# Four GNN layers on one core: where the first attention stripes' row work runs, layer 0's row buffers, and the order of the roots

## The chip, the cores and the metric

The kernel runs on one core of a Trainium2 chip. The metric is device time in microseconds (us), the median of three executions. Next to the times there is one execution recorded by the hardware profiler. Its engines are PE (TensorE, matmuls), DVE (VectorE), ACT (ScalarE), POOL (GpSimd) and SP (SyncE, which here issues the loads of the adjacency matrix). L1119 means line 1119 of the kernel.

## The reference

N = 4096 nodes with D = 64 features and a dense 0/1 adjacency matrix of float32. Four layers, each followed by a residual sum and a layer norm over the features:

```python
# layer 0
deg = clip(sum(adj, 1) + 1, 1)
h = (adj @ x + x) / deg
z = relu(concat([x, h]) @ W + b)
out0 = z / max(norm(z), 1e-12)
# layers 1 and 3 (c = 1 / r**2 in layer 1, c = 1 in layer 3)
x_t = logmap0(x, c)
left, right = x_t @ w_att[:D], x_t @ w_att[D:]
a = sigmoid(left[:, None] + right[None, :] + b_att) * adj
out = proj(expmap(x, einsum('ij,ijd->id', a, logmap(x[:, None], x[None], c))))
# layer 2: the last 100 neighbours of a row, weighted 0.5 ** (rank from the end)
out2 = w @ (x @ weight) + bias
# after each layer
x = layernorm(x + out, eps=1e-5)
```

So every attention layer needs, per pair of nodes (i, j), a sigmoid and a function of the distance in the hyperbolic space, and per node some scalars: squared norms, reciprocals, roots and logarithms.

## The kernel before

The nodes stand in 4 groups of 1024 (`GROUPS`, worked from 3 down to 0) and 32 blocks of 128. The adjacency matrix is streamed in tiles of 1 MB, `edges`, 256 of them, from SP into a pool of six buffers. Layers 0 and 2 are matmuls of edges with node features, with PE's and ACT's order written out by hand (`manual_schedule`). In the attention layers (1 and 3) that order is left to the scheduler, which keeps close to the order of the program.

**An attention stripe** (`attend`, L1064) is one group of target nodes against all 32 blocks. The blocks come in 16 pairs, highest first, and each block is a tile of 128 x 1024 scores. For one tile PE writes six matmuls into one of three PSUM buffers `z` (L1098, L1101, L1104), ACT makes a sigmoid `sig` (L1113) and a square `sq` (L1116), and DVE makes `t = max(z, 0) * sig` (L1119). For a pair DVE then makes `t = (sq + H²) * t` (L1121, 128 x 2048), and two pairs later PE adds t up with the features of the blocks (`acc`, L1076). At a stripe's end ACT copies acc out as `sums` (L1127).

**Row work** is what is done per node: 1024 nodes are a tile of 128 x 8 x 64, that is 128 x 512 features or 128 x 8 scalars. It is written as generators whose steps are issued between the tiles: `tick(n)` (L616) lets queued generators go on, and a generator that yields k rests for k ticks. The tick rate per tile is 2 in the first stripe of layer 1, 4 in the first stripe of layer 3, and 1 elsewhere, with one more call per pair. `need` (L643) runs ticks until a group is ready, before the first pair that reads it. How many ticks a generator rests is told by helpers: `soon`, `near`, `after(small)` and `pool_done`.

A layer's last group (group 0) is finished while the next layer's first stripe is already running on the blocks of groups 3, 2 and 1; so for layers 1 and 3 the following runs inside that first stripe: `end_0` (L1408) or `end_2` (L1540), which end layer 0 or 2; then `norm_rows` (L894), the layer norm; then `prepare` (L914), which makes the scalars and the operands of attention. `prepare` computes `y` (features scaled), its two-part representation in f16 (`ys`, `yd`), `xe` (the operand of L1076), then four transposes on PE (L978), each followed by a copy by ACT (L982) into `hi_lo`, `lo_hi`, `src` and `dst`; then two logarithms by ACT (L986, L987, which need another activation table than the sigmoid), a product on PE with the attention vectors (L991), and `left` and `right`. In attention the PSUM pool of these transposes (`aux`) has a single buffer.

**Roots** are computed from a bit trick and three Newton steps. `rsqrt` (L720) is on DVE: 1 + 3 x 3 instructions on 128 x 8. The class `Small` (L733) holds scalar row work that runs on DVE or on GpSimd; its `rsqrt` (L757) takes 1 + 3 x 3 on DVE, or the seed on DVE and 3 x 4 on GpSimd. The work at the end of each attention stripe (`move`, L1137) uses it.

**Buffers.** Pool `row` holds row tiles by name, one buffer each unless told otherwise. In layer 0 `own` holds the operands `first` and `third`, the sums of layer 0's own rows `xw`, the weights `sum_w` and `count_w`, and the scratch tile `junk`; a pool `m0_sb` holds `top` and `low`, copies of layer 0's sums. Both are closed at the end of layer 0, and the attention pool `p_sb` (sq, t, sig) then takes the same part of SBUF. A pool that takes another's place waits, through the dependences of its bytes, for the readers of what stood there.

Of the kernel before, what the change touches and what calls it, by code (L numbers as in the profile page):

```python
# [10 lines left out]
F32 = mybir.dt.float32  # L11
# [39 lines left out]
LN2 = 0.6931471805599453  # L51
ROOT2 = 2.0**0.5
LOG = (0.3333341, 0.1998662, 0.14984541)
OFF_EDGE = 255.0
# [6 lines left out]
def gnn_stack_kernel(  # L61
# [509 lines left out]
    def stream(fits):  # L571

        with ExitStack() as st:
# [89 lines left out]
            def pool_done(small, large=0):  # L663
# [3 lines left out]
                return 2 + int(small * 0.33 + large)  # L667

            spare, turn_of = [], [0]

# [49 lines left out]
            def rsqrt(a, name):  # L720

                n = a.shape[1]
                r, t = nums(name, n), nums("rs_t", n)
                V.tensor_scalar(
                    r.bitcast(I32), a.bitcast(I32), -0.5, float(0x5F3759DF), ALU.mult, ALU.add
                )
                for _ in range(3):
                    V.tensor_mul(t, r, r)
                    V.scalar_tensor_tensor(t, t, -0.5, a, ALU.mult, ALU.mult)
                    V.scalar_tensor_tensor(r, t, 1.5, r, ALU.add, ALU.mult)  # L730
                return r

            class Small:  # L733
# [23 lines left out]
                def rsqrt(self, a, name, small):  # L757

                    r, t = self.nums(name), self.nums("rs_t")
                    if self.on_pool:  # L760
                        yield self.wait(small)
                    V.tensor_scalar(
                        r.bitcast(I32), a.bitcast(I32), -0.5, float(0x5F3759DF),
                        ALU.mult, ALU.add,
                    )
                    for _ in range(3):
                        self.mul(t, r, r)
                        if self.on_pool:
                            self.mul(t, t, a)
                            self.ts(t, t, -0.5, 1.5, ALU.mult, ALU.add)  # L770
                            self.mul(r, t, r)
                        else:
                            self.stt(t, t, -0.5, a, ALU.mult, ALU.mult)
                            self.stt(r, t, 1.5, r, ALU.add, ALU.mult)
                    return r
# [39 lines left out]

            def att_rows(w_att, name):

                t = row.tile([1, 2, 2, D], F32, name=name + "_row")
                src = w_att.rearrange("(u d) o -> o u d", u=2)
                nc.scalar.dma_start(t, src[:, :, None, :].to_broadcast([1, 2, 2, D]))  # L820
                return t
# [72 lines left out]
            def norm_rows(layer, s, v, x2_to):  # L894

                m, v2, sq = nums("n_m"), nums("n_v2"), grp("sq")
                V.tensor_reduce(m, v, AX.X, ALU.add)
                V.tensor_scalar(m, m, 1.0 / D, None, ALU.mult)
                yield soon()
                V.tensor_sub(v, v, over(m))  # L900
                nc.gpsimd.tensor_mul(sq, v, v)  # L901
                yield soon()
                yield soon()
                V.tensor_reduce(v2, sq, AX.X, ALU.add)
                yield soon()
                V.tensor_scalar(m, v2, 1.0 / D, 1e-5, ALU.mult, ALU.add)
                r = rsqrt(m, "n_r")
                yield soon()
                V.tensor_mul(x_of(layer)[:, blocks(s), :], v, over(r))
                V.tensor_mul(x2_to, r, r)  # L910
                V.tensor_mul(x2_to, x2_to, v2)
                yield soon()

            def prepare(layer, s, att, b_att, curve, least, good, small):  # L914
# [4 lines left out]
                xg, bg, rbg = x_of(layer)[:, at, :], b[:, at], rb[:, at]  # L919
                V.tensor_scalar(cx2[:, at], x2[:, at], c, None, ALU.mult)  # L920
                V.tensor_scalar(bg, cx2[:, at], -1.0, 1.0, ALU.mult, ALU.add)
                V.reciprocal(rbg, bg)

                V.tensor_scalar(rbg, rbg, -0.13, 0.0, ALU.max, ALU.min)

                ym, y = nums("ym"), grp("y")
                V.tensor_scalar(ym, rbg, sc, None, ALU.mult)
                V.tensor_mul(y, xg, over(ym))

                def second():  # L930
# [12 lines left out]
                    for k, of in ((7, 0), (8, 0), (9, 1)):  # L943
                        nc.gpsimd.tensor_scalar(
                            ed[:, :, k], hl[:, :, of], -2.0 / UNIT, None, ALU.mult
                        )
                    V.tensor_sub(ys[:, :, D : 2 * D], y, ys[:, :, :D])

                    m, g, w = nums("m"), nums("g"), grp("xw")
                    V.tensor_scalar(g, cx2[:, at], 1.0, 1.0 / D, ALU.add, ALU.mult)  # L950
                    V.tensor_scalar(m, rbg, CUBE / UNIT, None, ALU.mult)
                    yield 1
                    V.tensor_add(w, xg, over(g))
                    yield 1
                    V.tensor_mul(xe[:, at, :], w, over(m))

                    q, q1, t = nums("q"), nums("q1"), nums("tt")
                    V.tensor_scalar(q, x2[:, at], least, c, ALU.max, ALU.mult)
                    V.tensor_scalar(q1, q, SMALL, None, ALU.max)
                    rt = rsqrt(q1, "rt")  # L960
                    V.tensor_mul(t, q1, rt)
                    V.tensor_scalar(t, t, TOP, None, ALU.min)
                    V.tensor_scalar(q1, q1, QTOP, None, ALU.min)
                    by_log = layer == 3 and s != GROUPS[-1]
                    if by_log:
                        half_log_of_ratio(t, q1)
                    yield 2 * near()
                    for into, rows_of in (
# [61 lines left out]

                later(second(), True, after(small))
                yield 1
# [321 lines left out]
            with ExitStack() as lp:  # L1354
                own = lp.enter_context(tc.tile_pool(name="m0_own", bufs=1))
                sb = lp.enter_context(tc.tile_pool(name="m0_sb", bufs=2))
                ps = lp.enter_context(tc.tile_pool(name="m0_ps", bufs=6, space=PSUM))
# [6 lines left out]
                third = own.tile([P, NB, D + 1], BF16, name="third")  # L1364
                xw = own.tile([P, NB, D], F32, name="xw")
                sum_w = own.tile([P, D + 1], F32, name="sum_w")
                count_w = own.tile([D + 1, D + 1], F32, name="count_w")
                ident_b = own.tile([P, P], BF16, name="ident_b")
# [32 lines left out]
                nc.scalar.dma_start(sum_w[:D, :D], w0[D:, :])  # L1401
                att_rows1, att_rows3 = att_rows(w_att1, "att1"), att_rows(w_att3, "att3")

# [4 lines left out]
                def end_0(s, tops):  # L1408
# [29 lines left out]
                    V.tensor_scalar(n2, n2, 1e-24, None, ALU.max)  # L1438
                    n = rsqrt(n2, "n")
                    yield 1  # L1440
                    V.tensor_mul(z, z, over(n))
                    V.tensor_add(z, z, x0[:, blocks(s), :])
                    yield 1
                    yield from norm_rows(1, s, z, x2[:, blocks(s)])
# [4 lines left out]
                with tc.manual_schedule(engines=FIXED):  # L1449
                    for s in GROUPS:  # L1450
# [37 lines left out]
                        for h in range(2):  # L1488
                            top = sb.tile([P, W], F32, name="top")
                            nc.scalar.copy(top, sums[h])  # L1490
                            low = sb.tile([D + 1, W], F32, name="low")
                            nc.scalar.copy(low, counts[h][: D + 1])
                            tops.append((top, low))
# [183 lines left out]
            with tc.manual_schedule(engines=FIXED):  # L1677
                spare.append(of_third)

                for some in (GROUPS[:2], GROUPS[2:3], GROUPS[3:]):  # L1680
                    accs = wide_pass(some) if len(some) == 2 else narrow_pass(some[0])
                    for s, of in zip(some, accs):
                        sums = [row.tile([P, W], F32, name="sums", bufs=2) for _ in of]
                        for to, acc in zip(sums, of):
                            nc.scalar.copy(to, acc)
                        later(end_2(s, sums))
# [98 lines left out]
```

## Time and profile before

| | us |
|---|---|
| median of 3 executions (1074.15 to 1074.6) | 1074.26 |
| the profiled execution | 1069.06 |
| its span on the core | 1067.3 |
| first score matmul of layer 1 | 185.02 |
| last stripe of layer 1 closed (L1127) | 517.38 |
| first score matmul of layer 3 | 714.08 |
| last stripe of layer 3 closed (L1127) | 1038.34 |

The mean granted clock of TensorE was 0.971 of full. Busy shares over the span, from the page's first part: PE 92%, DVE 86%, ACT 71%, POOL 25%. A share is an average over four stages with different limits, so stages are read one by one below. In a profile's timeline each line has the start, the duration, the engine, the line of the kernel, the operation, out<-in with shapes, how often it is repeated, and in brackets how long the engine stood idle before it and who released it.

```profile
PE   5997998789999999999999999998899999999980
DVE  8577887899999999999485489849999999999976
POOL 0011212010044515435500010101102454444163
PEclk8899999989999999999999999999999999999985
```

These are busy tenths in 40 slices of 26.7 us. Slices 7 to 19 (from 0) are layer 1's attention, 26 to 38 layer 3's. In the first stripe of each, GpSimd has almost nothing to do; in the other stripes it works on the rows of the stripe before.

### The profile page before, as it was taken

To read this page: it belongs to the slowest core of one execution; us is meant where nothing else is said; L and a number is where in the kernel's file an instruction comes from. 1 tells how busy PE (TensorE), PEld (TensorE's weight loads), DVE (VectorE), ACT (ScalarE), POOL (GpSimd) and SP (SyncE) were. 2 spreads that over 40 slices of the span, in tenths; PEclk is the share of its full clock that TensorE was granted. 3 is DMA by queue.
4 is the path that set the end of the run, shared out by engine and by line. 5 is a ranking of instruction groups with operands and counts; after the bars stand their busy time and mean duration, and the time that the engine had idled before them with its cause. 6 is when DMAs were issued, how large, how long until landed. Compare 5 with 4: busy or idle time off the path is not lost.

```text
span 1067.3 us, 13569 instructions
## 1 busy us (share of the span) xinstructions
PE 982.1 (92%) x4760; PEld 403.2 (38%) x4845; DVE 920.2 (86%) x1501; ACT 754.3 (71%) x877; POOL 270.8 (25%) x649
## 2 busy tenths in 40 slices
PE   5997998789999999999999999998899999999980
PEld 2454554333333333333333344443333333333320
DVE  8577887899999999999485489849999999999976
ACT  0013122779988899888677788898898888898850
POOL 0011212010044515435500010101102454444163
PEclk8899999989999999999999999999999999999985
DMA  9999999745656656757598999996465766666300
GB/s 364 356 426 364 383 395 375 277 175 197 233 204 230 215 206 202 249 184 249 205 363 332 371 346 316 324 321 222 138 236 190 250 216 208 241 228 234 131 1 24
DMA packets 38580, 271.62 MB, mean 254 GB/s; under 512 B 4710, under 2 KB 4710, under 8 KB 5734
## 3 DMA queue, kind: packets, MB, share of 16 engines
q1 hardware_dynamic: 37728, 270.03, 69.3%
q8 instruction: 40, 0.66, 0.2%
q10 hardware_dynamic: 774, 0.63, 0.2%
q14 instruction: 38, 0.31, 0.1%
HBM read 269.58 MB, written 1.05 MB: 254 GB/s over the span
## 4 chain that ended last, share of the span: by engine, by line
PE 66%; DVE 22%; ACT 5%; DMA 2%; POOL 2%; issue 2%; ACTq 0%; SPq 0%; POOLq 0%
PE acc L1076 17%; PE z L1641 11%; PE z L1101 8%; PE z L1098 7%; PE z L1104 7%; DVE t L1119 7%; DVE t L1121 6%; PE acc L1465 6%; PE z L1653 3%; DVE junk L844 2%; PE z L1607 2%; DMA edges<-in_adj_dram 2%; ACT sq L1648 1%; ACT sq L1116 1%; POOL sq L1435 1%
## 5 line engine op out<-in xcount | busy, mean ns | idle before, releaser
L1119 DVE SCALAR_TENSOR_TENSOR t<-z,sig 128x1024 f32<-128x1024 f32 x256 | 309.7, 1218 | 16.9 <-ACT sq L1116 14.9
L1121 DVE SCALAR_TENSOR_TENSOR t<-sq,t 128x2048 f32<-128x2048 f32 x128 | 295.2, 2306 | 0.2
L1116 ACT ACTIVATE sq<-z 128x1024 f32<-128x1024 f32 x256 | 254.3, 1021 | 56.5 <-PE z L1104 21.6
L1113 ACT ACTIVATE sig<-left_b,right 128x1024 f32<-128x1024 f32 x256 | 286.9, 1149 | 5.3 <-DVE t L1119 4.5
L1076 PE MATMUL acc<-t,xe 128*64 128x512 f32 x1024 | 260.4, 614 | 10.9 <-DVE t L1121 9.3
L1101 PE MATMUL z<-lo_hi,hi_lo 128*128 128x512 f16 x512 | 193.7, 378 | 3.8 <-issue 0.9
L1104 PE MATMUL z<-dst,src 74*128 74x512 f16 x512 | 194.7, 380 | 0.0
L1098 PE MATMUL z<-edges,two_i 128*128 128x512 bf16 x463 | 181.7, 392 | 5.4 <-DVE t L1119 5.4
L1648 ACT ACTIVATE sq<-z 128x512 bf16<-128x512 f32 (+1 forms) x192 | 137.6, 740 | 40.1 <-PE z L1641 39.5
L1076 PEld LDWEIGHTS acc<-t,xe 128*64 128x64 f32 x1024 | 64.3, 137 | 140.6 <-issue 106.5
L1098 PEld LDWEIGHTS <-two_i 128*128 128x128 bf16 x512 | 50.2, 98 | 120.7 <-issue 74.5
L1465 PE MATMUL acc<-edges,first 128*128 128x512 bf16 x241 | 77.9, 400 | 16.5 <-DMA edges<-in_adj_dram 15.9
L1641 PE MATMUL z<-edges,pass_by 128*128 128x512 bf16 x240 | 84.7, 388 | 7.3 <-ACT sq L1648 6.0
L844 DVE SCALAR_TENSOR_TENSOR t<-edges 128x2048 bf16<-128x2048 f32 x32 | 73.0, 2287 | 19.6 <-DMA edges<-in_adj_dram 19.2
L1641 PE MATMUL z<-edges,enter 128*128 128x512 bf16 x251 | 86.8, 387 | 0.5
L844 DVE SCALAR_TENSOR_TENSOR junk<-edges 128x2048 bf16<-128x2048 f32 x32 | 73.1, 2284 | 13.1 <-DMA edges<-in_adj_dram 13.1
L1465 PE MATMUL acc<-edges,third 128*65 128x512 bf16 x256 | 80.9, 397 | 0.8 <-issue 0.2
L1104 PEld LDWEIGHTS <-src 74*128 74x128 f16 x512 | 49.1, 96 | 72.0 <-issue 9.2
L1101 PEld LDWEIGHTS <-hi_lo 128*128 128x128 f16 x512 | 50.2, 98 | 60.6 <-issue 14.5
L901 POOL TENSOR_TENSOR sq<-z 128x512 f32<-128x512 f32 x8 | 10.2, 1278 | 156.1 <-DVE z L900 144.8
L1184 POOL TENSOR_TENSOR w_att<-x,u 128x512 f32<-128x512 f32 x6 | 12.7, 2121 | 140.9 <-ACT u L1179 140.9
L1607 PE MATMUL z<-sq,halves 128*128 128x512 bf16 x120 | 45.1, 377 | 0.7 <-ACT sq L1648 0.5
(399 smaller groups left out, 965.0 us busy)
## 6 DMA issues: line engine op xcount, KB each, us to landing
edges<-in_adj_dram SPq DMA_DIRECT2D x256, 1024.0 KB, 4.9
x<-in_x_dram SPq DMA_DIRECT2D x4, 256.0 KB
out_dram<-x ACTq DMA_DIRECT2D x2, 256.0 KB
out_dram<-x SPq DMA_DIRECT2D x2, 256.0 KB
w_sb<-in_L_gnn_W_dram ACTq DMA_DIRECT2D x1, 32.0 KB, 4.8
w_twice<-in_L_gnn_weight_dram ACTq DMA_DIRECT2D x2, 16.0 KB, 4.8
given<-in_L_gnn_b_dram ACTq DMA_DIRECT2D x1, 0.2 KB
given<-in_L_gnn_bias_dram ACTq DMA_DIRECT2D x1, 0.2 KB
```

The source lines that it names most:

```text
L844: V.scalar_tensor_tensor(junk, a, 0.0, a, ALU.not_equal, ALU.not_equal, accum_out=odd[:, n : n + 1])
L1076: it = nc.tensor.matmul(acc[h * D : (h + 1) * D, :], xe[:, j, :], t[:, k, h * W : (h + 1) * W], start=j == BLOCKS[0], stop=j == BLOCKS[-1],)
L1098: nc.tensor.matmul(half, two_i, edge[:, at : at + W], start=True, stop=False)
L1101: nc.tensor.matmul(half, hi_lo[:, of], lo_hi[:, to], start=False, stop=False)
L1104: last = nc.tensor.matmul(half, src[:, of], dst[:, to], start=False, stop=True)
L1113: nc.scalar.activation(sig, left_b, AF.Sigmoid, bias=right[:, j : j + 1])
L1116: nc.scalar.activation(sq[:, k], zp, AF.Square, bias=ROOT + OFF, scale=-1.0 / UNIT)
L1119: V.scalar_tensor_tensor(t[:, k], zp, 0.0, sig, ALU.max, ALU.mult)
L1121: V.scalar_tensor_tensor(t, sq, HIGH**2, t, ALU.add, ALU.mult)
L1465: nc.tensor.matmul(accs[h][:m], lhs[:, j, :], edge[:, at : at + W], start=j == BLOCKS[0], stop=j == BLOCKS[-1],)
L1641: nc.tensor.matmul(z[:, h : h + W], lhs, rhs[:, h : h + W], start=j == BLOCKS[0], stop=True, skip_group_check=True,)
L1648: weighed[0] = nc.scalar.activation(w, z[:, :n], AF.Exp, bias=-(OFF_EDGE + CUT) * LN2, scale=-LN2)
```

## The change

There are four edits.

1. Layer 0's row buffers: `xw` lies in the tile `halves`, `sum_w` and `count_w` in the pool that is never closed, `top` and `low` in row tiles (`sums`, `w_att`, `u_1`), the attention vectors' row in the tile `xw` of `row`. Pool `m0_sb` is gone.
2. For the last group, `end_0`, `norm_rows` and `prepare` issue on GpSimd most of the 128 x 512 steps and many scalar steps, and use the root of `Small` on GpSimd. New rests `far(small, large)` stand where the results are used.
3. All roots take one step of third order and one Newton step: 1 + 7 instructions on DVE, the seed on DVE and 10 on GpSimd.
4. Layer 2's sums of the last group are copied by DVE rather than ACT.

```diff
+THIRD = 0.375**0.5
...
+            def far(small, large=0):
+                beat = {1: 0.8, 3: 0.4}.get(place[0], 1.6)
+                return 1 + int((small * 0.29 + large * 1.04 + 2.3) / beat)
...
             def rsqrt(a, name):
-                for _ in range(3):
-                    V.tensor_mul(t, r, r)
-                    V.scalar_tensor_tensor(t, t, -0.5, a, ALU.mult, ALU.mult)
-                    V.scalar_tensor_tensor(r, t, 1.5, r, ALU.add, ALU.mult)
+                V.tensor_mul(t, r, r)
+                V.scalar_tensor_tensor(t, t, THIRD, a, ALU.mult, ALU.mult)
+                V.scalar_tensor_tensor(t, t, -10.0 / 3.0 * THIRD, t, ALU.add, ALU.mult)
+                V.scalar_tensor_tensor(r, t, 5.0 * THIRD**2, r, ALU.add, ALU.mult)
+                V.tensor_mul(t, r, r)
+                V.scalar_tensor_tensor(t, t, -0.5, a, ALU.mult, ALU.mult)
+                V.scalar_tensor_tensor(r, t, 1.5, r, ALU.add, ALU.mult)
...
             class Small:
...
                 def rsqrt(self, a, name, small):
...
+                    if self.on_pool:
+                        s = self.nums("rs_s")
+                        self.mul(t, t, a)
+                        self.ts(s, t, 0.375, -1.25, ALU.mult, ALU.add)
+                        self.mul(t, t, s)
+                        self.ts(t, t, 1.875, None, ALU.add)
+                        self.mul(r, t, r)
                         self.mul(t, r, r)
+                        self.mul(t, t, a)
+                        self.ts(t, t, -0.5, 1.5, ALU.mult, ALU.add)
+                        self.mul(r, t, r)
...
             def norm_rows(layer, s, v, x2_to):
...
+                pooled = s == GROUPS[-1]
+                E = nc.gpsimd if pooled else V
                 yield soon()
-                V.tensor_sub(v, v, over(m))
+                E.tensor_sub(v, v, over(m))
                 nc.gpsimd.tensor_mul(sq, v, v)
-                yield soon()
-                yield soon()
+                if pooled:
+                    yield far(0, 2)
+                else:
+                    yield soon()
+                    yield soon()
...
-                r = rsqrt(m, "n_r")
-                yield soon()
-                V.tensor_mul(x_of(layer)[:, blocks(s), :], v, over(r))
-                V.tensor_mul(x2_to, r, r)
-                V.tensor_mul(x2_to, x2_to, v2)
-                yield soon()
+                if pooled:
+                    r = yield from Small(True, "").rsqrt(m, "n_r", 0)
+                else:
+                    r = rsqrt(m, "n_r")
+                    yield soon()
+                E.tensor_mul(x2_to, r, r)
+                E.tensor_mul(x2_to, x2_to, v2)
+                E.tensor_mul(x_of(layer)[:, blocks(s), :], v, over(r))
+                if not pooled:
+                    yield soon()
...
             def prepare(layer, s, att, b_att, curve, least, good, small):
...
-                V.tensor_scalar(cx2[:, at], x2[:, at], c, None, ALU.mult)
-                V.tensor_scalar(bg, cx2[:, at], -1.0, 1.0, ALU.mult, ALU.add)
+                E.tensor_scalar(cx2[:, at], x2[:, at], c, None, ALU.mult)
+                E.tensor_scalar(bg, cx2[:, at], -1.0, 1.0, ALU.mult, ALU.add)
+                if pooled:
+                    yield far(14, 1)
                 V.reciprocal(rbg, bg)
-                V.tensor_scalar(rbg, rbg, -0.13, 0.0, ALU.max, ALU.min)
+                E.tensor_scalar(rbg, rbg, -0.13, 0.0, ALU.max, ALU.min)
-                V.tensor_scalar(ym, rbg, sc, None, ALU.mult)
-                V.tensor_mul(y, xg, over(ym))
+                E.tensor_scalar(ym, rbg, sc, None, ALU.mult)
+                E.tensor_mul(y, xg, over(ym))
...
-                    V.tensor_sub(ys[:, :, D : 2 * D], y, ys[:, :, :D])
+                    E.tensor_sub(ys[:, :, D : 2 * D], y, ys[:, :, :D])
-                    V.tensor_add(w, xg, over(g))
-                    V.tensor_mul(xe[:, at, :], w, over(m))
+                    E.tensor_add(w, xg, over(g))
+                    E.tensor_mul(xe[:, at, :], w, over(m))
...
-                    rt = rsqrt(q1, "rt")
-                    V.tensor_mul(t, q1, rt)
-                    V.tensor_scalar(t, t, TOP, None, ALU.min)
-                    V.tensor_scalar(q1, q1, QTOP, None, ALU.min)
+                    if pooled:
+                        rt = yield from Small(True, "").rsqrt(q1, "rt", 0)
+                    else:
+                        rt = rsqrt(q1, "rt")
+                    E.tensor_mul(t, q1, rt)
+                    E.tensor_scalar(t, t, TOP, None, ALU.min)
+                    E.tensor_scalar(q1, q1, QTOP, None, ALU.min)
-                    yield 2 * near()
+                    yield far(10, 1) if pooled else 2 * near()
...
-                later(second(), True, after(small))
+                later(second(), True, far(2, 1) if pooled else after(small))
...
                 own = lp.enter_context(tc.tile_pool(name="m0_own", bufs=1))
-                sb = lp.enter_context(tc.tile_pool(name="m0_sb", bufs=2))
-                xw = own.tile([P, NB, D], F32, name="xw")
-                sum_w = own.tile([P, D + 1], F32, name="sum_w")
-                count_w = own.tile([D + 1, D + 1], F32, name="count_w")
+                xw = halves.bitcast(F32)
+                sum_w = keep.tile([P, D + 1], F32, name="sum_w")
+                count_w = keep.tile([D + 1, D + 1], F32, name="count_w")
...
                 def end_0(s, tops):
...
-                    n = rsqrt(n2, "n")
-                    yield 1
-                    V.tensor_mul(z, z, over(n))
-                    V.tensor_add(z, z, x0[:, blocks(s), :])
-                    yield 1
+                    if s == GROUPS[-1]:
+                        n = yield from Small(True, "").rsqrt(n2, "n", 0)
+                        nc.gpsimd.tensor_mul(z, z, over(n))
+                        nc.gpsimd.tensor_add(z, z, x0[:, blocks(s), :])
+                        yield far(10, 2)
...
-                            top = sb.tile([P, W], F32, name="top")
+                            top = row.tile([P, W], F32, name="sums", bufs=2)
...
                         for to, acc in zip(sums, of):
-                            nc.scalar.copy(to, acc)
+                            if s == GROUPS[-1]:
+                                V.tensor_copy(to, acc)
+                            else:
+                                nc.scalar.copy(to, acc)
```

## The prediction

> **What bounds the kernel now.** I read the page first (busy times, chain, groups), then the ACT timeline at each end of a stripe, then DVE, ACT, PE and POOL side by side over the two first attention stripes (185–287 and 714–810 us), and last the end of the program.
>
> ```profile
> PE 66%; DVE 22%; ACT 5%; DMA 2%; POOL 2%; issue 2%; ACTq 0%; SPq 0%; POOLq 0%
> ...
> L1119 DVE SCALAR_TENSOR_TENSOR t<-z,sig 128x1024 f32<-128x1024 f32 x256 | 309.7, 1218 | 16.9 <-ACT sq L1116 14.9
> L1121 DVE SCALAR_TENSOR_TENSOR t<-sq,t 128x2048 f32<-128x2048 f32 x128 | 295.2, 2306 | 0.2
> ```
>
> The chain runs over PE and DVE. In a steady attention stripe they are level: a pair of tiles costs DVE two L1119 (start to start 1.13) and one L1121 (2.20), 4.46 us, and PE twelve matmuls of 0.22 and 1.87 for L1076, about 4.6 us. So in attention anything put into DVE's or PE's order is paid for, unless the stripe has slack. How much the first stripes lose is read from the copies that close stripes one and two of layer 1, and one and two of layer 3:
>
> ```profile
> 287.05 0.58 ACT L1127 COPY sums<-acc 128x512 f32<-128x512 f32 x1
> ...
> 364.09 0.59 ACT L1127 COPY sums<-acc 128x512 f32<-128x512 f32 x1
> ...
> 809.77 0.59 ACT L1127 COPY sums<-acc 128x512 f32<-128x512 f32 x1
> ...
> 886.49 0.59 ACT L1127 COPY sums<-acc 128x512 f32<-128x512 f32 x1
> ```
>
> A steady stripe takes 77.0 and 76.7 us, 2.4 a tile. The first ones, from their first score matmul (185.02 and 714.08), take 102.0 and 95.7 for about 36 tiles' worth, some 86. So about 16 and 10 us are excess, and only these can be won in attention. Where they lie in layer 1:
>
> ```profile
> 189.31 1.28 ACT L1113 ACT_TABLE_LOAD   x1 [5.31 <-DVE z L1429]
> ```
> ```profile
> 194.93 0.39 PE L1098 MATMUL z<-edges,two_i 128*128 128x512 bf16 x1 [3.72 <-DVE t L1119]
> ...
> 229.57 0.62 PE L978 MATMUL aux<-ident,ys 128*128 128x128 f16 x8 [1.96 <-DVE ys L947]
> 231.29 1.01 PE L978 MATMUL aux<-ident,ys 128*128 128x128 f16 x8 [1.10 <-ACT hi_lo L982]
> ```
> ```profile
> 242.10 0.21 DVE L1001 TENSOR_REDUCE lr<-aux 128x16 f32<-128x48 f32 x1 [3.71 <-PE aux L991]
> ```
>
> The first: ACT stands 5.31 us before its first sigmoid, whose buffer lies where layer 0's xw lay, which DVE's L1429 reads. The others: PE waits for scores, then for the last group's row batch (225.81 to 229.90 on DVE), and the transposes go one by one through a single buffer that ACT empties.
>
> The price of GpSimd is in the POOL timeline of a later stripe:
>
> ```profile
> 311.67 0.20 POOL L771 TENSOR_TENSOR r_t<-rs_t,r_t 128x8 f32<-128x8 f32 x1
> 311.95 2.24 POOL L767 TENSOR_TENSOR rs_t<-r_t 128x8 f32<-128x8 f32 x1
> 314.26 0.20 POOL L769 TENSOR_TENSOR rs_t<-rs_t,t 128x8 f32<-128x8 f32 x1
> ...
> 363.40 1.04 POOL L1266 TENSOR_TENSOR u<-u,q 128x512 f32<-128x512 f32 x1
> 364.52 3.11 POOL L1269 TENSOR_TENSOR x<-u,w_att 128x512 f32<-128x512 f32 x1
> ```
>
> A small operation takes 0.20 (0.28 to the next), but 2.24 when it meets L1121 on DVE; a large one 1.04, or 3.11.
>
> **What the Trainium skill says.** "SBUF — State Buffer", Who interferes with whom: a DVE instruction with two SBUF inputs and a GpSimd instruction that reads SBUF exclude each other, whoever starts first. The trace agrees: L1121 (both inputs in SBUF) gives the 2.24, L1119 (z in PSUM) does not. So GpSimd loses some 2.2 of every 4.6 us, and L1121 can be held by a large GpSimd operation too (3.16 instead of 2.28 at 363.43). "GPSIMD Engine Reference", 3.1 Elementwise: an add takes 1.96 times as long as on DVE; here 1.04 against 0.69, 1.5 times.
>
> **The change, part by part.** Times are of the profiled execution (1069.06; span 1067.3, 1.8 around it). The median 1074.26 is 5.2 above it; I keep that distance.
>
> *Layer 0's buffers.* The sigmoid buffers no longer overlie what L1429 reads. ACT's last copy ends at 184.0, the table load (1.28) at 185.3, the first sigmoid at 186.35, the square at 187.3. DVE's order still has z's finish (to 189.1) ahead of the first L1119, so that goes from 193.66 to 189.1, 4.5 earlier; the root's ten instructions (191.76 to 193.58) are no longer ahead of it. The other overlays (junk, first) are read earlier; I take no new wait from them.
>
> *Last group on GpSimd, layer 1.* In DVE's new order three of its instructions wait for GpSimd with scores queued behind them: the mean's sum (L897 before), the variance's sum (L904) and the reciprocal (L922); further on the attention factor (L1006) waits for ACT's logarithm, whose input now comes from a GpSimd root. DVE is in order, so each late result stops the scores, and through them PE. Writing u1, u2, ... for the L1121s and stepping with 1.13, 2.20, 0.08 (small) and 0.60 (large):
> u1 192.45 (before 197.85), u2 197.9 (205.15). The root is seeded at 196.0: six of its ten GpSimd steps fit before u2, the seventh waits to 200.1, three more to 201.0, then two large ones to 203.1. DVE comes free at 201.3, so the mean's sum stops it 1.9. u3 206.2 (211.19). The subtract and square stop it 0.9: u4 212.35 (215.89), u5 216.8 (220.59). The next root meets u4 and u5 (2.8 + 2×2.0), then x, x2 and 1−cx² (0.28 each, 1.04 for x): the reciprocal waits until 221.3, 2.4 idle; u6 223.2 (229.90). Before, DVE's batch cost 4.1 there. The low half of ys comes from GpSimd at 229.25 behind u6; PE's transposes therefore wait at 227.3–229.3, as before. u7 229.2 (233.54), u8 234.35 (242.50); the transposes now lie between four tiles, so the 3.71 stop goes, while the logarithm and its two table loads (245.57–249.4 before) come at about 241–244. u9 241.6 (247.41). The twentieth L1119 ends at 248.0 against 252.63: **−4.6**. So the 4.5 of the buffers survives, and moving row work nets about nothing: about 7.8 us of DVE work go (one root 2.0, two spread ones 0.8 each, seven large ones of 0.6), and 5.2 of stops, transposes held for ys and steps that DVE did while it would have waited for PE anyway come.
>
> *Last group on GpSimd, layer 3.* Here no buffer wait is won; ticks are twice as dense, so the same waits come after fewer tiles. DVE's sums copies (two, 0.6 each) and the bias add that waits for PE stand ahead of the first L1119: 719.1 against 718.67. u1 722.9 (722.36); subtract and square stop DVE 1.2; u2 730.6 (728.09). The root needs 2.8 plus a 2.0 block, then about six more operations before the reciprocal: stop 3.5, u3 737.6 (735.52). The low half of ys (742.0–743.05) holds u4: 743.05 (740.22). u5 749.2 (744.91), u6 752.75 (750.21). The third root meets both, ACT's logarithm waits to 756.5, DVE behind it 2.7: u7 763.05 (757.72). Then it gains: the batch of 4.1 is gone and transposes are past. At u10's tile it is 780.1 against 778.4: **+1.7**.
>
> *Third order.* Seven dependent steps after the seed instead of nine on DVE, ten instead of twelve on GpSimd. In the tail's chain three DVE roots stand in a row with 0.20 a step:
>
> ```profile
> 1047.16 0.90 DVE L767 TENSOR_TENSOR rs_t<-r_t 128x8 f32<-128x8 f32 x1
> ...
> 1055.33 0.17 DVE L767 TENSOR_TENSOR rs_t<-n 128x8 f32<-128x8 f32 x1
> 1055.53 0.17 DVE L747 SCALAR_TENSOR_TENSOR rs_t<-rs_t,mt 128x8 f32<-128x8 f32 x1
> ```
>
> 3×2×0.20 = 1.2, and half of one GpSimd root at 1037–1042 (2×0.28, of which ACT's copy at 1042.4 lets 0.3 through): **−1.5**. The three steps stretched to 0.9–1.0 by GpSimd's L1265–L1269 remain. In layer 0 (DMA busy share 0.92 to 0.99) and layer 2 (PE) shorter roots are hidden: 0, at most −0.5. In steady stripes a root sheds at most 2 of 0.08 from DVE: below 0.3.
>
> *Sums by DVE.* ACT gives up 2×0.5 at 716.66, but is not late there: 0 beyond the 0.4 counted.
>
> Sum −4.6 + 1.7 − 1.5 = −4.4: span 1062.9, profiled 1064.7, median 1069.9. Unknown costs: a GpSimd result may slip before or behind one L1121, 2.2 each way, at the seven or so waits of the two stripes; a net of two in one direction is ±4, which I take.
>
> **Rivals.**
> (1) GpSimd hides better: its operations fall between the L1121s and the layer 3 stops (1.2 + 3.5 + 2.7) shrink to half. For: GpSimd stands idle from 202 to 227 now. Against: the groups are dependent chains longer than the 2.4 us gap. −4.4 − 3.7: about 1066. 15%.
> (2) In-order DVE behind blocked GpSimd, the slower side: one more 2.2 block at the reciprocal and at the factor in both stripes, +8.8, PE idle with its clock dropping to 0.8 as at 220–240. For: every root is longer than a gap. Against: before also had a 3.7 stop there that goes. −4.4 + 8.8: 1078.7. It decides from 6.5 us of added stops. 13%.
> (3) The buffers do not free ACT: another overlay (junk, the first operand) still orders the first sigmoid behind layer 0's end. Then 0 + 1.7 − 1.5, within 0.2% (2.15 us, about what a measurement can tell from no change): 1074.5. Against: the profile names L1429 alone. 15%.
>
> **How the numbers follow.** Forecast 57%, own range 1067.5–1073; rivals 15, 13, 15%. The range 1066 to 1077 takes in (1)'s value and (3), and reaches towards (2). Faster by over 0.2% (below 1072.1): nearly all of (1), most of the forecast: 0.70. Within: 0.17. Slower: (2), 0.13.
>
> **What would show it.** Table load at 184 instead of 189.31 and first L1119 near 189.1; first stripe's closing copy near 282.4, the second stripe still 77.0 later; in layer 3 95.7 + 1.7 us; DVE idle with POOL as releaser about 5 us in layer 1 and 7 in layer 3; from the last closing copy to the end 1.5 shorter than 29.0 us. Wrong if stripes two to four change by over 1 us, if the first L1119 stays near 193, or if POOL stops sum to over 18 us.

## The result and the profile after

| | before | changed |
|---|---|---|
| median of 7 executions each, side by side | 1074.06 (1070.35 to 1074.6) | 1069.25 (1064.74 to 1074.99) |
| ratio, 95% interval | | 0.9972 [0.9948, 0.9996] |
| profiled execution, span | 1069.06, 1067.3 | 1068.74, 1067.0 |

The change is faster by 0.28%, and the interval's upper end, 0.9996, is nearly no change. The forecast, 1069.9, is met by the median; the profiled pair differs by only 0.3 us. So the stages have to be read one by one. Lines have moved: in the changed kernel L1160 and L1162 are L1119 and L1121 of before, L1117 is L1076, L1139 is L1098 and L1019 is L978; in the other kernels they are a few lines off these. The chain of the changed kernel has moved from DVE to PE and GpSimd:

```profile
PE 70%; DVE 16%; ACT 5%; POOL 4%; DMA 4%; issue 2%; ACTq 0%; SPq 0%; POOLq 0%
```

The copies that close stripes one and two of layer 1, and one and two of layer 3 (ACT timeline):

```profile
286.77 0.59 ACT L1168 COPY sums<-acc 128x512 f32<-128x512 f32 x1
...
363.75 0.59 ACT L1168 COPY sums<-acc 128x512 f32<-128x512 f32 x1
...
810.83 0.59 ACT L1168 COPY sums<-acc 128x512 f32<-128x512 f32 x1
...
887.81 0.59 ACT L1168 COPY sums<-acc 128x512 f32<-128x512 f32 x1
```

The first score matmuls stand at 182.92 and 713.19. From there the first stripes take 103.9 us (before 102.0) and 97.6 (95.7); the second ones 77.0 each (77.0 and 76.7). From layer 3's first closing copy to the end it is 256.2 instead of 257.5. Layer 1 did not gain its 4.6 (its first closing copy stands at 286.77, not near 282.4), although the wait that was to go is gone, as the ACT timeline shows:

```profile
181.92 1.28 ACT L1154 ACT_TABLE_LOAD   x1
...
191.55 1.02 ACT L1157 ACTIVATE sq<-z 128x1024 f32<-128x1024 f32 x1 [4.18 <-PE z L1145]
```

The table load has no idle time before it (5.31 before). But the second square now waits 4.18 us for PE, whose granted clock is 0.50 just there, from 184 to 190 us of this execution (PE timeline; the same matmul takes 0.39 at full clock, 0.63 here):

```profile
182.92 0.39 PE L1139 MATMUL z<-edges,two_i 128*128 128x512 bf16 x1
...
183.73 0.63 PE L1139 MATMUL z<-edges,two_i 128*128 128x512 bf16 x1
```

After that come the forecast stops of DVE (its timeline: mean's sum, variance's sum, reciprocal, each released by POOL), and then one that was priced too low (PE timeline: the first transposes wait for the low half of ys, and the next sums of L1117 take 3.22 us for eight matmuls, not 1.94):

```profile
205.78 0.69 DVE L920 TENSOR_REDUCE n_m<-z 128x8 f32<-128x512 f32 x1 [1.86 <-POOL z L1482]
...
211.94 0.69 DVE L932 TENSOR_REDUCE n_v<-sq 128x8 f32<-128x512 f32 x1 [0.93 <-POOL sq L926]
...
224.06 0.20 DVE L958 RECIPROCAL rb<-b 128x8 f32<-128x8 f32 x1 [2.23 <-POOL b L955]
```
```profile
231.03 1.03 PE L1019 MATMUL aux<-ident,ys 128*128 128x128 f16 x8 [4.15 <-POOL ys L983]
232.00 3.22 PE L1117 MATMUL acc<-t,xe 128*64 128x512 f32 x8
```

Layer 3 shows its stops where the forecast put them (DVE timeline), and the third root on GpSimd held by two L1162s (POOL timeline, its usual 0.20 grown to 2.36), with the low half of ys at 3.20:

```profile
726.40 0.69 DVE L932 TENSOR_REDUCE n_v<-sq 128x8 f32<-128x512 f32 x1 [1.22 <-POOL sq L926]
...
736.52 0.20 DVE L958 RECIPROCAL rb<-b 128x8 f32<-128x8 f32 x1 [3.70 <-POOL b L955]
...
756.57 0.17 DVE L1050 SCALAR_TENSOR_TENSOR f<-q,tt 128x8 f32<-128x8 f32 x1 [1.87 <-ACT q L1028]
```
```profile
741.27 3.20 POOL L983 TENSOR_TENSOR ys<-y,ys 128x512 f16<-128x512 f32 x1 [0.73 <-DVE hl L971]
...
752.32 2.36 POOL L786 TENSOR_TENSOR rt<-rs_t,rt 128x8 f32<-128x8 f32 x1
```

### The profile page after: what moved, and what is told of

Same layout as the page of the kernel before. It is cut to its first block, busy times and chain, and to the rows that moved or that the text cites. A ratio compares the mean times of both kernels' runs of the same rounds, so it can differ in the third digit from the quotient of the medians.

```text
span 1067.0 us, 13581 instructions
## 1 busy us (share of the span) xinstructions
PE 986.4 (92%) x4845; PEld 402.8 (38%) x4845; DVE 902.7 (85%) x1380; ACT 753.0 (71%) x875; POOL 305.6 (29%) x695
## 4 chain that ended last, share of the span: by engine, by line
PE 70%; DVE 16%; ACT 5%; POOL 4%; DMA 4%; issue 2%; ACTq 0%; SPq 0%; POOLq 0%
PE acc L1117 18%; PE z L1693 11%; PE z L1139 9%; PE z L1145 8%; PE z L1142 8%; PE acc L1511 5%; DVE t L1160 4%; DVE t L1162 4%; DMA edges<-in_adj_dram 3%; PE z L1705 3%; PE z L1659 2%; DVE junk L867 2%; ACT sq L1700 1%; ACT sq L1157 1%; PE aux L1209 1%
## 5 line engine op out<-in xcount | busy, mean ns | idle before, releaser
L1160 DVE SCALAR_TENSOR_TENSOR t<-z,sig 128x1024 f32<-128x1024 f32 x256 | 309.9, 1219 | 21.1 <-ACT sq L1157 18.5
L1162 DVE SCALAR_TENSOR_TENSOR t<-sq,t 128x2048 f32<-128x2048 f32 x128 | 295.2, 2306 | 0.3
L1117 PE MATMUL acc<-t,xe 128*64 128x512 f32 x1024 | 258.9, 615 | 13.9 <-DVE t L1162 13.0
L1139 PE MATMUL z<-edges,two_i 128*128 128x512 bf16 x512 | 201.4, 393 | 5.9 <-DVE t L1160 5.9
L1117 PEld LDWEIGHTS acc<-t,xe 128*64 128x64 f32 x1024 | 63.8, 137 | 144.3 <-issue 103.8
L1511 PE MATMUL acc<-edges,first 128*128 128x512 bf16 x256 | 80.3, 395 | 16.5 <-DMA edges<-in_adj_dram 16.2
L1139 PEld LDWEIGHTS <-two_i 128*128 128x128 bf16 x512 | 50.6, 99 | 117.4 <-issue 71.9
L1659 PE MATMUL z<-sq,halves 128*128 128x512 bf16 x128 | 48.1, 377 | 0.6 <-ACT sq L1700 0.6
## 6 DMA issues: line engine op xcount, KB each, us to landing
x<-in_x_dram SPq DMA_DIRECT2D x4, 256.0 KB
out_dram<-x ACTq DMA_DIRECT2D x2, 256.0 KB
out_dram<-x SPq DMA_DIRECT2D x2, 256.0 KB
```

The source lines that it names most:

```text
L1117: it = nc.tensor.matmul(acc[h * D : (h + 1) * D, :], xe[:, j, :], t[:, k, h * W : (h + 1) * W], start=j == BLOCKS[0], stop=j == BLOCKS[-1],)
L1139: nc.tensor.matmul(half, two_i, edge[:, at : at + W], start=True, stop=False)
L1160: V.scalar_tensor_tensor(t[:, k], zp, 0.0, sig, ALU.max, ALU.mult)
L1162: V.scalar_tensor_tensor(t, sq, HIGH**2, t, ALU.add, ALU.mult)
L1511: nc.tensor.matmul(accs[h][:m], lhs[:, j, :], edge[:, at : at + W], start=j == BLOCKS[0], stop=j == BLOCKS[-1],)
```

## The experiments

Theory: the steps of the prediction, buffers −4.5, handover neutral in layer 1 and costly in layer 3. Rival: in layer 1 the handover gives back what the buffers win. Each ratio is to the kernel before, timed beside it. Since layer 0's end alone lies anywhere from 182.9 to 190.6 us in the profiled executions, the table counts stripes from the first score matmul, each in one profiled execution. Rows with the same code in a stage show the scatter of that stage.

In brackets stands how much of a stripe PE spent at half clock. The granted clock is 1.00 or 0.50 in these stretches, so a slice of 1 us with a mean of 0.75 counts as 0.5 us.

| kernel | ratio to before, 95% | first stripe, layer 1 (of it at half clock) | first stripe, layer 3 (of it at half clock) | from there to the end |
|---|---|---|---|---|
| before | 1 | 102.0 (10.2) | 95.7 (3.4) | 257.5 |
| changed | 0.9972 [0.9948, 0.9996] | 103.9 (17.1) | 97.6 (3.4) | 256.2 |
| buffers alone | 1.0013 [0.9993, 1.0032] | 101.1 (3.4) | 95.4 (3.4) | 257.7 |
| roots alone | 0.9965 [0.9950, 0.9980] | 102.4 (13.7) | 96.1 (3.4) | 255.9 |
| buffers and roots | 0.9938 [0.9920, 0.9957] | 98.7 (3.4) | 95.9 (3.4) | 255.9 |
| no handover | 0.9913 [0.9889, 0.9937] | 99.9 (6.8) | 93.2 (0) | 256.0 |
| handover in layer 1 | 0.9949 [0.9930, 0.9967] | 100.9 (10.2) | 94.4 (6.8) | 256.0 |
| handover in layer 3 | 0.9963 [0.9949, 0.9978] | 97.2 (0) | 97.3 (10.2) | 256.2 |
| end_0 only | 0.9891 [0.9872, 0.9909] | 98.0 (6.8) | 95.7 (6.8) | 255.8 |
| low half back | 0.9905 [0.9881, 0.9930] | 95.4 (0) | 95.7 (3.4) | 256.0 |
| low half alone | 0.9945 [0.9920, 0.9970] | 99.2 (3.4) | 95.6 (6.8) | 256.1 |
| low half back, layer 1 | 0.9899 [0.9864, 0.9935] | 98.0 (6.8) | 94.4 (3.4) | 256.0 |
| second half, layer 1 | 0.9981 [0.9956, 1.0005] | 106.7 (17.1) | 94.1 (3.4) | 255.9 |
| second half, both | 1.0032 [1.0014, 1.0050] | 103.3 (10.2) | 100.1 (13.6) | 255.8 |

**Buffers alone.** Edit 1 on the kernel before.

> The kernel before with edit 1 alone (layer 0's row buffers). Theory of the prediction: ACT's first sigmoid no longer waits, first L1119 near 189 instead of 193.66, and the gain lasts: the first stripe of layer 1, from its first score matmul to its closing copy, takes about 97.5 instead of 102.0 us, layer 3's stays at 95.7, the end at 29.0; total -4.5 us against before (ratio about 0.996). Rival (the gain is taken back in the same stripe by the row batch and the serial transposes, which then come at an earlier tile): stripe 101 to 102, total within 1 us of before.

The first stripe took 101.1 and the ratio is 1.0013: the theory's 97.5 did not come. The early part is as expected: the first L1119 (L1123 in this kernel) follows the first score matmul by 4.1 us instead of 8.6. Then the gain is lost at one place (ACT timeline; the logarithm, its copies of `left` for the next stripe, and the way back to the sigmoid):

```profile
258.19 1.28 ACT L990 ACT_TABLE_LOAD   x1
259.48 0.21 ACT L990 ACTIVATE tt<-tt 128x8 f32<-128x8 f32 x1
...
261.45 0.59 ACT L1064 COPY left_b<-aux 128x512 f32<-128x512 f32 x1 [1.66 <-PE aux L1058]
...
263.65 0.59 ACT L1064 COPY left_b<-aux 128x512 f32<-128x512 f32 x1 [0.52 <-PE aux L1058]
264.25 1.28 ACT L1117 ACT_TABLE_LOAD   x1
```

ACT does no sigmoid from 253 to 265.5, and DVE stands 4.29 us before its next L1123. In ACT's order the logarithm stands behind the 24th sigmoid here, behind the 19th in the kernel before: the scores went ahead and the rows, a root step per tile, did not, so the logarithm ran into the next stripe's `left`.

**No handover, and handover in one layer.**

```diff
-                pooled = s == GROUPS[-1]
+                pooled = False
...
-                    if s == GROUPS[-1]:
+                    if False:
```

In the kernels for one layer the first condition has `and layer == 1` or `and layer == 3` instead, and end_0's own belongs to layer 1.

> The changed kernel without edit 2: the last group's rows stay on VectorE in both attention layers; buffers, third-order roots and sums by VectorE stay. Theory of the prediction (handover neutral in layer 1, +1.7 in layer 3): layer 1's first stripe as in the changed kernel within 1 us, layer 3's 95.7 instead of 97.6, end 27.6; total 2 us below the changed kernel. Rival (in layer 1 the handover gives back what the buffers win): layer 1's first stripe about 98 instead of 103.9, so 5 to 7 us below the changed kernel, ratio to before about 0.993.

> The changed kernel with edit 2 in layer 1 only. Theory of the prediction: layer 1's first stripe as in the changed kernel, layer 3's 95.7, total 2 us below the changed kernel, and equal to the kernel without handover. Rival (handover costs in layer 1): about 4 us above the kernel without handover, stripe near 103.

> The changed kernel with edit 2 in layer 3 only. Theory of the prediction: equal to the changed kernel, layer 3's first stripe 97.6. Rival (handover costs in layer 1): 4 us below the changed kernel, with layer 1's first stripe near 98 and layer 3's still 97.6.

Without the handover the kernel is at 0.9913, and its interval and the changed kernel's do not overlap: GpSimd's share of the change costs about 0.6%, some 6 us.

In layer 3 the loss is shown. The kernel with the handover there alone (0.9963) does not overlap with the one without it, and the stripe takes 97.6 and 97.3 with it, 93.2 to 95.7 in the five kernels that have edits 1, 3 and 4 and leave layer 3's rows to VectorE. At the same 3.4 us of half clock it is 97.6 against 94.4 and 94.1.

In layer 1 it is not settled. The stripes look as the rival said: 99.9, 97.2 and 98.7 (mean 98.6) in the three kernels with no handover there, 103.9 and 100.9 (102.4) in the two with it. But the ratios of handover in layer 1 and of no handover just overlap (0.9930 and 0.9937), those of changed and of handover in layer 3, which also differ by it alone, overlap widely, and the stripes differ in their time at half clock.

Kernels with the same code in layer 1 differ by 0.4 to 0.5 us for each us at half clock: 103.9 and 100.9 with 17.1 and 10.2, 99.9, 98.7 and 97.2 with 6.8, 3.4 and 0, 98.0 and 95.4 with 6.8 and 0, 106.7 and 103.3 with 17.1 and 10.2. With 0.43 us taken off for each, 96.5 and 96.5 are left with the handover and 97.0, 97.2 and 97.2 without. So by this estimate the loss in layer 1 is time at half clock, and apart from that the handover is about neutral there, as the theory had it. Not all of that time is the handover's: 10.2 of the changed kernel's 17.1 us lie in the first 11 us of the stripe, and roots alone, which has no handover, shows the same 10.2 there. But over all executions the changed kernel did run at a lower clock: its mean granted clock is 0.968 to 0.977 in seven (mean 0.974), 0.977 to 0.983 in six of no handover (0.980).

**Roots alone, buffers and roots.** Edit 3 on the kernel before, and edits 1 and 3; the second is no handover with `nc.scalar.copy(to, acc)` for all of layer 2's sums.

> The kernel before with edit 3 alone (roots of third order). Theory of the prediction: only the end gains, 1.3 to 1.5 us, ratio 0.9987; both first stripes as before (102.0 and 95.7). Rival formed after the first runs (roots stand one step per tile in VectorE's order, so two steps fewer bring the last group's rows to the transposes two tiles sooner): layer 3's first stripe about 93.5 to 94.5, layer 1's 101 or less, end -1.4; ratio 0.996 or lower.

> The kernel before with edits 1 and 3 (buffers and roots), without the handover and with layer 2's last sums copied by ScalarE. If the sums by VectorE are worth nothing: equal to the kernel without handover (ratio to before 0.991, layer 3's first stripe 93.2). Rival (the sums by VectorE give layer 3 its 2 us): layer 3's first stripe 95.4, ratio 0.993. If edits 1 and 3 simply add up, the ratio is that of buffers alone (1.001) times that of roots alone; if they need each other, it is lower than this product.

The end gains 1.6 to 1.7 us in both. Alone the roots bring 0.35%, but neither first stripe of the one profile is shorter than before, so the rival's place for it is not shown, and the 2 us beyond the end stay open; in layer 1 this one execution spent 13.7 us at half clock. The product with the buffers would be 0.9978; together they reach 0.9938. In ACT's order the logarithm is now behind the 22nd sigmoid, before the copies of `left`, and the first stripe takes 98.7. This fits edit 1 paying only where the row chain is short enough to end before the next stripe's preparation, but does not show it: the intervals of roots alone and of both together overlap by a hair (0.9950 and 0.9957), and with half clock taken off as above the stripe is 97.2 with both and 96.5 with the roots alone. The sums by VectorE are worth little: layer 3 takes 95.9 without them, 93.2, 94.4 and 95.7 with them and no handover there; the ratios' intervals overlap, and it stays open.

**Low half back, low half alone.** One instruction, in two surroundings: back on VectorE in the changed kernel, or alone on GpSimd without the rest of the handover.

```diff
-                    E.tensor_sub(ys[:, :, D : 2 * D], y, ys[:, :, :D])
+                    V.tensor_sub(ys[:, :, D : 2 * D], y, ys[:, :, :D])
```

The kernel with it alone is no handover with:

```diff
-                    E.tensor_sub(ys[:, :, D : 2 * D], y, ys[:, :, :D])
+                    (nc.gpsimd if s == GROUPS[-1] else V).tensor_sub(
+                        ys[:, :, D : 2 * D], y, ys[:, :, :D]
+                    )
```

> The changed kernel with one instruction of the handover, the low half of ys, back on VectorE. Theory (PE's 4.15 us wait for ys from GpSimd is the main cost of the handover in layer 1, and what follows on a lowered clock): layer 1's first stripe 2 to 4 us below the 103.9 and 100.9 of the two kernels with the handover, ratio to before near 0.994. Rival (the costs are VectorE's stops at the sums and the reciprocal, 5.0 us together): nothing changes, 0.997.

> The kernel without handover with one instruction moved: the low half of ys of the last group on GpSimd, in both attention layers. Theory (this one instruction, between y and PE's transposes, is the dear one): PE's wait for ys grows from 1.7 to 2 to 4.5 us, PE's clock falls in 235 to 245 us, layer 1's first stripe 2 to 4 us above the 97.2 to 99.9 of the kernels without it, layer 3's 1 to 2 above 94.4; ratio to before 0.994 to 0.996. Rival (it is dear only behind the other GpSimd work of the whole handover): within 1 us of the kernel without handover, 0.991.

With it back, the ratio falls from 0.9972 to 0.9905, again without overlap: this one instruction costs some 7 us in the two layers. Layer 1's first stripe falls to 95.4. The first transposes of low half back do not wait, and PE's clock stays full. But the full clock is not the instruction's doing. Low half back in layer 1 has the same code in layer 1, its transposes do not wait for ys either, and yet it falls to half clock there (PE timelines, first of low half back, then of low half back in layer 1):

```profile
226.78 0.62 PE L1019 MATMUL aux<-ident,ys 128*128 128x128 f16 x8
```
```profile
228.23 3.68 PE L1117 MATMUL acc<-t,xe 128*64 128x512 f32 x8 [1.60 <-DVE t L1162]
231.84 1.03 PE L1019 MATMUL aux<-ident,ys 128*128 128x128 f16 x8
```

The three window lines, 225 to 235 us, are of the changed kernel, of low half back, and of low half back in layer 1. Behind the stretch and its length they give busy time and instructions of PE, PEld, DVE, ACT and POOL, then the granted clock, DMA share and GB/s:

```profile
225.00:235.00 10.00, 5.45 (x22) 2.02 (x21) 9.74 (x13) 6.58 (x8) 9.68 (x14) 0.66 0.07 29
```
```profile
225.00:235.00 10.00, 9.93 (x67) 4.56 (x69) 9.96 (x12) 9.99 (x12) 8.13 (x21) 1.00 0.50 173
```
```profile
225.00:235.00 10.00, 8.09 (x29) 2.99 (x30) 10.00 (x14) 6.63 (x9) 9.39 (x15) 0.66 0.04 16
```

PE does 67 pieces of work in these 10 us where the changed kernel does 22, but only 29 where the clock is as low as in the changed kernel, so most of this difference is the clock. With half clock taken off as above, the stripes of layer 1 are 95.4 and 95.1 with the low half on VectorE, 96.5 with it on GpSimd: an estimate of some 1.2 us for the wait itself. Layer 3's stripe goes from 97.6 to 95.7 at the same 3.4 us of half clock. The rest of the 7 us is not located; the mean granted clock over whole executions is 0.976 to 0.982 with the low half back and 0.968 to 0.977 without. VectorE's stop at the reciprocal is the same in both (2.22 against 2.23), so the 7 us are not its doing. Alone on GpSimd the instruction makes PE wait 3.00 instead of 1.70, here from low half alone and from no handover:

```profile
239.40 1.04 PE L1021 MATMUL aux<-ident,ys 128*128 128x128 f16 x8 [3.00 <-POOL ys L983]
```
```profile
237.47 0.62 PE L1019 MATMUL aux<-ident,ys 128*128 128x128 f16 x8 [1.70 <-DVE ys L983]
```

Its stripes, 99.2 and 95.6, lie within the scatter of those without it; the ratio is 0.3% higher, but the intervals overlap, so whether it costs anything alone is not settled. PE's clock over 235 to 245 us is 0.83 with it and 0.66 in no handover, so the expected fall through it did not come. In the changed kernel it comes late: on GpSimd a copy that meets L1162 (2.21 us; 0.24 in layer 3) and a 128x512 step (1.04) stand ahead of it, and PE does nothing meanwhile. That only this makes it dear is argued, not shown, as the ratio of low half alone overlaps with the changed kernel's too.

**Better versions.** End_0's part only (root n and two large steps of layer 1; `pooled = False` in both other places); the handover in layer 1 with the low half on VectorE (`pooled = s == GROUPS[-1] and layer == 1` beside the edit of low half back); and end_0 with the later part of `prepare` on GpSimd (xw, xe, root rt and what follows), in layer 1 or in both. The last are end_0 only with the edit of low half back and, against the changed kernel:

```diff
+                    behind = s == GROUPS[-1] and layer == 1
+                    F = nc.gpsimd if behind else V
...
-                    E.tensor_add(w, xg, over(g))
...
+                    F.tensor_add(w, xg, over(g))
...
-                    E.tensor_mul(xe[:, at, :], w, over(m))
+                    F.tensor_mul(xe[:, at, :], w, over(m))
...
-                    if pooled:
+                    if behind:
                         rt = yield from Small(True, "").rsqrt(q1, "rt", 0)
```

> The changed kernel with only end_0's part of the handover (root n and two large steps in layer 1); norm_rows and prepare stay on VectorE in both layers. If the loss sits in the wait for these (1.86 us at the mean's sum): layer 1's first stripe 2 us above the kernel without handover, ratio 0.993. Rival (the loss sits in norm_rows and prepare): equal to the kernel without handover, 0.991, or below it by the ten root steps that leave VectorE.

> The handover in layer 1 only, with the low half of ys on VectorE. If the parts add up: layer 1's first stripe 95.4, layer 3's 93.2 to 95.7 as in the kernels without handover there, ratio 0.989. Rival: the 95.4 was an execution with a full clock only; stripe 98 to 99, ratio 0.991.

> In layer 1 only: end_0's part of the handover, and from prepare only what nothing waits for at once (xw, xe, the root rt and what follows it); norm_rows, y and the low half of ys stay on VectorE. Theory (only steps between the layer norm and the transposes are dear on GpSimd): VectorE's stop of 2.2 at the reciprocal is gone, layer 1's first stripe 94 to 96, ratio 0.988 or lower. Rival (the scores lose to VectorE's longer spread of the n_r root): as with end_0's part alone, 98.0 and 0.989.

> As the last, with the same part of prepare on GpSimd in layer 3 too. Theory: layer 3's first stripe falls below 94.4, by the four large steps and the root (2 us at most): 92.5 to 94, ratio 0.987. Rival (GpSimd's chain to the logarithm comes late, as in the changed kernel where ScalarE's logarithm stood early): 95 to 96, ratio 0.989.

End_0 only and low half back in layer 1 are at 0.9891 and 0.9899, the fastest measured: 1.1% and 1.0% below the kernel before. They, low half back and no handover are not told apart by their intervals; end_0's part costs nothing, as its rival had it. The 95.4 of low half back was partly a good execution: the same code of layer 1 took 98.0 in the other kernel, with 6.8 us at half clock instead of none. The second half's theory fell, and the traces say why (DVE, then PE, of second half in layer 1):

```profile
243.52 0.30 DVE L1041 TENSOR_SCALAR m<-b,k_of_y 128x8 f32<-128x8 f32 x1 [3.41 <-POOL xe L995]
```
```profile
245.10 0.58 PE L1141 MATMUL z<-edges,two_i 128*128 128x512 bf16 x1 [4.49 <-DVE t L1162]
```

The scalar tile `m` is first a factor of xe and is then written again by DVE. With xe on GpSimd that write waits for GpSimd's read, and the next scores and the low half of ys stand behind it in DVE's order. I had called these steps ones that nothing waits for; the reused tile waits. Layer 1 takes 106.7 here and 103.3 in second half in both, which has the same code in layer 1 and 6.9 us less at half clock. With the edit in both layers the kernel is slower than before (1.0032).

## Why the prediction was right, and where it was not

**The whole: right by luck.** The forecast −4.4 lies inside the measured interval (−0.4 to −5.6 us at 1074), and near the medians' −4.8. But it is the sum of two errors that cancel. Without the handover the ratio 0.9913 is −9.3 us, where the forecast had −4.6 for layer 1's buffers and −1.5 for third order; the handover then takes back some 6.3 of it (together −3.0 by the ratio), where the forecast had 1.7. In the profiled pair layer 1's first stripe went +1.8, layer 3's +1.9, the end −1.4, layer 0 −2.1, and the other stages −0.6; layer 0's part is within what it varies.

**The buffers: right wait, wrong worth.** The wait for L1429 went. That the first L1160 stands at 189.16, as worked out (189.1), is chance: layer 0 ended 2.1 us earlier and PE ran at half clock, so it follows the first score matmul by 6.2 us; in buffers alone it is the expected 4.1. Rival (3), another overlay, is excluded, though its zero came true by another way, as the buffers alone are worth nothing (1.0013). The step that failed is that the early start would last: what is late next was not looked for beyond the stops. It was the logarithm and the copies of `left`. Beside shorter roots the same edit may be worth some 3 us (0.9938 against 0.9965), by intervals that overlap a little.

**The handover in layer 1: the failed terms.** "PE's transposes therefore wait at 227.3–229.3, as before" had 2.0 us; it was 4.15, and 4.14 in handover in layer 1. The three stops of DVE were sized well (1.9, 0.9 and 2.4 against 1.86, 0.93 and 2.23). The term that was to net about nothing cost 3.8 by the means of the stripes (102.4 less 98.6), so −4.6 became +1.8 in the one profile and −1.1 in handover in layer 1. What the steps left out is PE's clock: the stripes with the handover have 13.7 us at half clock on average, those without 3.4, and by the estimate above that accounts for all of the 3.8.

"TensorE: Matmul & The Clock Gate", What's actually happening, says that an idle window of some 3.4 us halves the clock. The trace agrees with the half and with the length: the clock was 0.50, eight matmuls of L1117 took 3.22 us, and every bracket of the table is a multiple of 3.4 us. It does not agree that PE must stand idle for so long: in the changed kernel the clock fell at 227.8, only 0.9 us after PE's last matmul had ended, with 1.5 us of work in the 3.4 us before; in low half back in layer 1 it fell at 227.4, 0.8 us into a stop of 1.60 that follows one of 1.55. Low half back has the same two stops and kept its full clock. So it did not take a wait of 4.15 us, and whether a stop takes the clock down differs between executions of the same code.

**Layer 3: right in the stops, too small in the sum.** +1.7 forecast, +1.9 measured, with stops of 1.22, 3.70 and 1.87 for 1.2, 3.5 and 2.7. Against the version without handover it loses more, some 3 us (97.5 against a mean of 94.4 over the five kernels without it); the other edits had gained some 1.3 there (95.7 to 94.4) that the forecast did not have. So the near hit is partly chance.

**Third order: right at the end, too small elsewhere.** −1.5 forecast; 257.5 to 256.2, and 255.8 to 256.2 in all kernels with it. For the other stages the forecast had next to nothing, while roots alone gain some 2 us more than the end. What it left out is the row chain of the first stripe, one root step per tile: two steps less move the logarithm two tiles forward (from behind the 24th sigmoid to the 22nd with the buffers, from the 19th to the 17th without). Whether the 2 us lie there is not shown.

**Sums by VectorE.** Costed at nothing; not told apart from it.

**The rivals.** Rival (2) had the right cause, in-order engines behind a blocked GpSimd, and alone named PE's falling clock, but put the late result at the reciprocal and the factor; the wait that was missed was at ys, in PE. Rival (1) is excluded by the stops.

## What to carry to other kernels

A step handed to a slower engine should be judged by who stands behind its consumer: one 128x512 step between y and PE's transposes, put back on VectorE, brought 0.7%, while VectorE's stop at the reciprocal stayed as it was. After removing a wait, follow the order to the next thing that is late, also in another engine's fixed order; an edit that gains nothing alone may still pay beside another. Before comparing single profiled executions of two kernels, compare their granted clock: in layer 1's first stripes it explains, by the estimate above, more than the edit. Before moving reads to another engine, look for small tiles that are written again: the write inherits the wait.

## What was not expected of the hardware

The length of a first stripe with the same code differs by some 3 us between executions (103.9 and 100.9, 99.9 and 97.2, 98.0 and 95.4), and goes with its time at half clock, 0.4 to 0.5 us for each us in layer 1. That time is 0, 3.4, 6.8, 10.2, 13.6 or 17.1 us in all the stripes of the table. Where it falls differs too: in the changed kernel PE's clock was low from 183.4 us, in low half back the start up to 200 us ran at full clock. A small DVE instruction that writes a scalar tile, 0.16 us elsewhere, took 1.04 (the seed of rt, second half in layer 1, at 236.77) while GpSimd ran a 128x512 step of 1.04 us at 236.74, so in this place the small instruction was the one that waited.
